# A gated cross-attention and feed-forward stack on one core: contexts loaded in whole rows, later places for two early pieces of work, smaller credits beside the attention steps

## The chip, the cores and the metric

The kernel runs on one core of a Trainium2 chip. A core has TensorE (PE, matrix products, with a path PEld that loads the fixed operand), VectorE (DVE), ScalarE (ACT), GpSimd (POOL) and SyncE (SP), and queues for DMA, which SyncE, ScalarE and GpSimd issue. The metric is the device time of one execution in microseconds (us). Three runs before the change took 3881.97, 3875.95 and 3877.2 us; the median is 3877.2. Lower is better.

## The reference

The input is x, 8 sequences of 512 tokens with 256 features, and a context of the same shape. Four blocks follow one another, each as x = x + tanh(gate) * block(layernorm(x)):

1. An mLSTM cell: queries from x, keys and values are the context itself, 8 heads of 32. Two gates come from small products of queries, keys and values. A cumulative sum of log-sigmoids gives a decay matrix; scores times decay weigh the context; a normalizer divides; a layernorm ends it.
2. Self-attention with 32 heads of 8 over each half sequence layout of the reference, then an output product, then eight experts (256 to 1024, GELU, back to 256), two per sequence here.
3. Cross-attention with 16 heads of 16: queries from x, keys and values projected from the context.
4. A product-key memory: 4096 experts found by two top-8 searches over 64 keys each; a chosen expert is one row of a down and an up table. The queries are batch-normalized over all tokens, so this block needs sums over the whole batch before it can choose.

The core of block 1, of which the context as keys and values (kh, vh) matters here:

```python
log_f = jax.nn.log_sigmoid(fg)
cs = jnp.cumsum(log_f, axis=1)
...
D_mat = jnp.exp(log_D - max_log_D)
qk = jnp.einsum('hsd,htd->hst', qh, kh) / np.sqrt(DH)
C = qk * D_mat
normalizer = jnp.maximum(jnp.abs(C.sum(axis=-1, keepdims=True)), jnp.exp(-max_log_D))
h = jnp.einsum('hst,htd->hsd', C / (normalizer + EPS), vh)
```

All is float32.

## The kernel before, in words

The first phase (`attention_phase`) does blocks 1 to 3 for all sequences; the second does block 4. TensorE's order is written out in the program and kept; in the first phase the other engines' orders are chosen by the framework's scheduler, which may bring an instruction forward when its model finds its inputs ready. A semaphore guards every true dependency.

**Steps.** The backbone of the first phase is a row of 24 attention jobs: ("A", m, f) is half f of the heads of block 2 for sequence m, ("C", m, 0) is block 3. A job has 16 steps, and a step two halves. In a half, `maxima` makes a pair of score products into a PSUM bank pair `sc` (line 417), VectorE reduces them to row maxima `nm` (line 435); for the job before it, `exponentials` makes the products the other way round, and ScalarE takes exp into `pr` (line 464). Once per step `values` multiplies by the values (line 480). Exponentials of a job begin when its maxima are closed, so two jobs run side by side, one step behind the other by a job; before the first exponentials, and in a few places later, one of the two runs alone. The score pool `ps_sc` has two buffers.

**Lanes.** Everything else of blocks 1 to 3 is cut into generators, the lanes. Between halves the planner runs pieces of lanes (`beside`): it is given a CREDIT (1.1 in the first half of a step, 2.1 in the second) and runs pieces while credit is left; what was overspent is taken off the next. A lane yields a number (the PE time of the piece it has written), or ("wait", t): not before the planner's clock `now` has moved by t, or ("rest", name): not before that name stands in `rested`, or ("take", ...) for the one accumulator bank. The clock moves after each turn by at least RETURN, 2.6 (3.9 for a step where one job runs alone, whose two halves are one turn), or by the work written. The lanes in order of precedence:
- `between` (operands of block 2's jobs: spreads of queries and keys from DRAM, lines 386 and 394, on SyncE), `values1`, `after` (leaves block 3, adds to the statistics, at the end `norm`);
- `before` for sequences 0, 2, 3, ...: `cell` (block 1) and `queries` (block 2's projections); and `behind`: `experts` and `operands` (block 3's queries); the two take turns;
- `before` for sequence 1, whose tiles are lent (`Lent`) from experts' weights, so that it runs next to the first; once the first step has begun it moves ahead of the two;
- `contexts`: block 3's keys (`keys3`, line 365 with wkv) and values (`values3`, line 376 with wkv), first for the first four sequences of the order, then for the others;
- `fill`: products of x with the down table for block 4, `ps_hd` (line 131, copied to `hb` at line 1190 and stored to `h_d`), 32 pieces a sequence, for seven sequences, each after its sequence has left block 3. The eighth sequence's products are made in the second phase.

**The start.** x of the first sequence is loaded, layernormed (lines 98 to 107; the reciprocal root `rs` is made on GpSimd, lines 103 and 104), transposed, and the gates' product `gp` (line 717) follows. A chain on VectorE and ScalarE makes the running maxima nM (to line 744), stored to DRAM (746) and read back spread over the partitions. The first sequence's cell (`all_pairs`) does all heads in a row: four such loads (line 625), a causal mask on GpSimd (638), decays on ScalarE (649), scores and their weighing (663, 669), sums with the context's keys `ce` (684), then `close` (768 to 783). Then come two layernorms, the result `xn` (888), its transposes (346), queries and keys of block 2 (365 with ws, copied at 905 and 907), its values (376, copied at 920), and through `begin` the first score.

**Context keys.** The cell's sums need the context as 8 heads of 33 columns, 32 features and a column of ones. The tile is set to ones once, and `load_keys` (line 223) loads 32 features to each head's place: per sequence four DMAs, whose contiguous pieces are 32 numbers, 128 bytes. The first sequence and sequence 1 issue them on SyncE, the other six on GpSimd.

**Waits around the change.** `Lent`'s lane loads its operands at once, and then rests on ("pairs", 0), which stands as soon as the first cell's pairs are written. `contexts` has no rest for its first half; its first piece waits 25 on the planner's clock. For its second half it rests on ("A", 1, 0).

Of the kernel before, what the change touches and what calls it, by code (L numbers as in the profile page):

```python
# [10 lines left out]
F32 = mybir.dt.float32  # L11
# [10 lines left out]
P = 128  # L22
B, S, D = 8, 512, 256
NC = S // P
# [12 lines left out]
def kernel(  # L37
# [27 lines left out]
    nc = tc.nc  # L65
# [57 lines left out]
    order = (0, 4, 1, 5, 2, 6, 3, 7)  # L123
# [56 lines left out]
    def attention_phase(ctx: ExitStack):  # L180
# [10 lines left out]
        cel, trp, wmp, wq1 = (  # L191
            early.enter_context(tc.tile_pool(name=name, bufs=bufs, side="right"))
            for name, bufs in (("cel", 2), ("trp", 1), ("wmp", 1), ("wq1", 2))
        )
# [11 lines left out]
        for c2 in range(2):  # L206
            part = slice(2 * c2, 2 * c2 + 2)
# [8 lines left out]
        cT0 = cxp.tile([P, NK, S], F32, name="cT", tag="cTc")  # L216
        nc.sync.dma_start(cT0, cxT[order[0]].rearrange("(k p) s -> p k s", p=P))
        cte = cst.tile([P, NC, WC], F32, name="cte")
        nc.gpsimd.memset(cte, 1.0)

        def load_keys(eng, ce, b):
            for c in range(NC):
                eng.dma_start(
                    ce[:, c, : 8 * 33].rearrange("p (h e) -> p h e", e=33)[:, :, 0:32],
                    cx[b, c * P : (c + 1) * P].rearrange("p (h e) -> p h e", e=32),
                )

        load_keys(nc.sync, cte, order[0])

        gwm = cst.tile([P, 4, 40], F32, name="gwm")  # L230
        nc.gpsimd.memset(gwm, 0.0)
        for i in range(2):
            part = slice(8 * i, 8 * i + 8)
# [75 lines left out]

        v0 = [cst.tile([P, NC, W0], F32, name=f"v0{f}") for f in range(2)]  # L310
        v1 = cst.tile([P, NC, W1], F32, name="v1")
        for f in range(2):
            nc.gpsimd.memset(v0[f], 1.0)
        nc.gpsimd.memset(v1, 0.0)


        m_u8 = cst.tile([B * NC, P], U8, name="m_u8")
# [3 lines left out]

        def constants():

            bo_ps = ps_m.tile([P, S], F32, name="bo_ps", tag="m")
            for k in range(NK):
                nc.tensor.matmul(
                    bo_ps[:, :D], bqkv_sb[:, 4 + k : 5 + k].to_broadcast([P, P]), wo[:, k, :],
                    start=(k == 0), stop=(k == NK - 1),
                )
            nc.vector.tensor_tensor(tbo, bo_ps[:, :D], tbo, ALU.add)  # L330
            nc.vector.tensor_scalar(tbo, tbo, tg[:, 2:3], None, ALU.mult)
            m_f = trp.tile([B * NC, P], F32, name="m_f", tag="pk", bufs=2)
            nc.vector.tensor_copy(m_f, m_u8)
            mp = ps_m.tile([P, S], F32, name="mp", tag="m")
            nc.tensor.transpose(mp[:, : B * NC], m_f, ident[: B * NC, : B * NC])
            nc.vector.tensor_copy(m_key, mp[:, : B * NC])
            nc.vector.tensor_scalar(m_f, m_f, 1.0, -NEG, ALU.subtract, ALU.mult)
            nc.sync.dma_start(m_dram, m_f)
# [211 lines left out]
        class Tiles:  # L550
# [9 lines left out]
            def begin(self, m):  # L560

                b = order[m]
                if m == 0:
                    return x0, cT0, cte
                qn = self.tokens("qn")
                self.loader.dma_start(qn, x[b].rearrange("(c p) d -> p c d", p=P))
                cT, ce = self.context(m)
                load_keys(self.loader, ce, b)
                return qn, cT, ce

            def context(self, m):
# [132 lines left out]
        def cell(m, own, loaded):  # L704
            b = order[m]
# [83 lines left out]

            if m == 0:  # L790
                all_pairs(qT, cT, ce, nM_d, aT, close)
                rested.add(("pairs", 0))
            for pair in range(4) if m else ():

                mb = own.maximum()
# [57 lines left out]
            Xa = own.stream()  # L853
# [176 lines left out]
        def contexts():  # L1030

            for half in (range(M // 2), range(M // 2, M)):
                for i in (1, 2):
                    if i == 1 and half[0]:
                        yield ("rest", ("A", 1, 0))
                    w = wsp.tile([P, NK, D], F32, name="wkv", tag="wkv")
                    nc.sync.dma_start(w, w3[i].rearrange("(k p) n -> p k n", p=P))
                    for m in half:
                        cT = load_context(m, "cT")
                        yield ("wait", 5 if m or i > 1 else 25)  # L1040
                        for cost in (keys3, values3)[i - 1](m, w, cT):
                            yield cost
                            yield ("wait", 2)
# [160 lines left out]

        LAG, CREDIT, GROUP, RETURN = 2, (1.1, 2.1), 1.1, 2.6

# [16 lines left out]
        def before(sequences, tiles):  # L1227
            own, loaded = tiles(), None
            if tiles is Lent:
                loaded = own.begin(sequences[0])  # L1230
                yield ("rest", ("pairs", 0))
            for m in sequences:
                Xa = yield from cell(m, own, loaded)
                yield from queries(m, own, Xa)
            if tiles is Lent:
                rested.add(("lent", 0))
                load_first(0)
                load_second(0)
# [106 lines left out]
        while i2 < len(steps) or pending or due:  # L1345
# [19 lines left out]
            for halves in ((0, 1),) if alone else ((0,), (1,)):  # L1365
# [18 lines left out]
                if halves[0] == 0 and pending:  # L1384
# [2 lines left out]
                        done = pending  # L1387
                    pending = None
                    used += GROUP
                new = sum(CREDIT[half] for half in halves)  # L1390
                spent = beside(credit + new)
                now += max(RETURN * (1.5 if alone else 1.0), used + new + credit - spent)
                credit = min(spent, CREDIT[1])
            if one:
                i1 += 1
                if one[1] == 15:
# [497 lines left out]
```

## Time and profile before

| what | value |
|---|---|
| median of three runs | 3877.2 us |
| profiled execution | 3878.41 us, span 3876.6 us, mean granted clock 0.966 |
| PE busy | 3534.1 us, 91% |
| DVE, ACT, POOL busy | 2247.1, 1755.9, 607.4 us |
| first score product of a step | 129.6 us |
| last exponentials | about 2937 us |
| last expert piece of the first phase | about 3015 us |
| DMA packets | 233643, of which 34558 under 512 bytes |

Times in the profile are counted from the span's start. The span is first to last instruction of the core; the profiled execution's own time is 1.8 us longer. A busy PE is modelled from instruction ends, and the granted clock tells how fast it was allowed to run: 1.00 is full, 0.50 half. A row of the timeline gives start, length, engine, line, operation, output and inputs with their shapes, how often, and in brackets the idle time before it and what ended it. SPq, POOLq and ACTq rows are DMA issues.

### The profile page before, as it was taken

What the parts mean: (1) busy time and instruction counts of PE and PEld (TensorE: products, weight loads), DVE (VectorE), ACT (ScalarE), POOL (GpSimd) and SP (SyncE); (2) the same over time, 40 slices, a digit from 0 to 9 for tenths busy, and PEclk for the clock granted to TensorE, in tenths of its full rate; (3) what the DMA queues carried; (4) which work ended last, traced back from release to release, by engine and by line L of the source; (5) the groups of instructions that cost most, each with busy time, mean ns of one, the idle gap of its engine ahead of it and who ended that gap; (6) DMA issues with size and microseconds to landing.
All of it is one profiled execution on the core that took longest, in us unless ns stands there. A gap on an engine that the chain in (4) does not pass through costs nothing. (4 is left out here: it accounts for less than half of the span.)

```text
span 3876.6 us, 76238 instructions
## 1 busy us (share of the span) xinstructions
PE 3534.1 (91%) x31049; PEld 1847.7 (48%) x31049; DVE 2247.1 (58%) x5487; ACT 1755.9 (45%) x2301; POOL 607.4 (16%) x647
## 2 busy tenths in 40 slices
PE   5788889899899999999999989979899899999998
PEld 3333334333334434443434434424345777777777
DVE  4556556546555554555554443454422589999993
ACT  2223444443444444545444544534343455555552
POOL 4113003003001200210010000010000133333331
PEclk8789999999999999999999999999999999999999
DMA  5413113123222422232232333211334432333331
GB/s 154 109 51 99 53 40 113 53 66 101 83 63 71 130 77 68 83 111 59 83 89 87 91 89 107 69 44 29 121 115 139 127 108 98 117 110 112 106 104 37
DMA packets 233643, 345.35 MB, mean 89 GB/s; under 512 B 34558, under 2 KB 182046, under 8 KB 224990
## 3 DMA queue, kind: packets, MB, share of 16 engines
q1 hardware_dynamic: 215196, 278.03, 24.3%
q0 software_dynamic: 16960, 61.87, 5.3%
q8 instruction: 244, 4.00, 0.4%
q10 hardware_dynamic: 1136, 0.58, 0.1%
q14 instruction: 107, 0.88, 0.1%
HBM read 238.50 MB, written 101.09 MB: 88 GB/s over the span
## 5 line engine op out<-in xcount | busy, mean ns | idle before, releaser
L435 DVE TENSOR_REDUCE nm<-sc 128x2 f32<-128x1024 f32 x768 | 938.9, 1225 | 988.8 <-PE sc L417 988.1
L464 ACT ACTIVATE pr<-sc 128x1024 f32<-128x1024 f32 x768 | 783.3, 1023 | 991.2 <-PE sc L417 990.7
L417 PE MATMUL sc<-ka,qa 32*128 32x512 f32 x3072 | 929.4, 667 | 155.7 <-DVE nm L435 146.5
L417 PE MATMUL sc<-qa,ka 32*128 32x512 f32 x3072 | 874.4, 655 | 16.3 <-ACT pr L464 14.6
L417 PEld LDWEIGHTS sc<-ka,qa 32*128 32x128 f32 x3072 | 253.9, 190 | 525.5 <-DVE nm L435 335.1
L1736 PE MATMUL acc<-up_sb,gs 64*128 64x256 f32 x4096 | 468.4, 382 | 1.3 <-DVE gs L1725 1.3
L131 PE MATMUL ps_hd<-xT,dw 128*64 128x256 f32 x3584 | 431.8, 387 | 11.4 <-DVE pd L839 5.3
L480 PE MATMUL av<-pr,v 128*32 128x512 f32 x3072 | 421.9, 622 | 0.0
L1736 PEld LDWEIGHTS acc<-up_sb,gs 64*128 64x128 f32 x4096 | 390.0, 187 | 52.4 <-issue 4.7
L131 PEld LDWEIGHTS ps_hd<-xT,dw 128*64 128x64 f32 x3584 | 247.6, 138 | 226.1 <-issue 86.2
L1706 POOL TENSOR_TENSOR m<-o,cwT 128x1024 f32<-128x1024 bf16 x128 | 243.6, 1903 | 583.1 <-DVE o L1704 261.2
L1190 ACT COPY hb<-ps_hd 128x512 f32<-128x512 f32 x224 | 130.9, 584 | 302.6 <-PE ps_hd L131 251.8
L417 PEld LDWEIGHTS sc<-qa,ka 32*128 32x128 f32 x3072 | 236.5, 186 | 56.0 <-ACT pr L464 41.8
L480 PEld LDWEIGHTS av<-pr,v 128*32 128x32 f32 x3072 | 61.2, 109 | 301.0 <-issue 301.0
L1725 DVE TENSOR_TENSOR gs<-cf,gs 128x1024 f32<-128x1024 f32 x128 | 155.5, 1216 | 42.3 <-PE cf L1716 27.4
L812 ACT ACTIVATE pd<-mb,aT 128x512 f32<-128x512 f32 (+1 forms) x224 | 113.3, 553 | 138.8 <-PE cav L819 71.7
L804 POOL TENSOR_SCALAR_AFFINE_SELECT mb<-mb 128x256 f32<-128x256 f32 x112 | 45.5, 407 | 781.5 <-ACT pd L812 413.5
L1716 PE MATMUL cf<-m,m 64*64 64x64 f32 x8192 | 152.9, 222 | 4.4 <-issue 3.6
L1716 PEld LDWEIGHTS cf<-m,m 64*64 64x64 f32 x8192 | 135.1, 135 | 42.6 <-issue 42.2
L1702 ACT CAST m<-o 128x1024 f32<-128x1024 bf16 x128 | 133.7, 1045 | 39.2 <-DVE o L1700 35.3
L834 PE MATMUL csc<-qT,cT 32*128 32x512 f32 (+1 forms) x448 | 125.0, 499 | 18.9 <-DVE o L508 6.0
L990 PE MATMUL ps_h<-fT,w1e 128*128 128x256 f32 x512 | 134.0, 396 | 5.8 <-DVE o L508 4.4
(260 smaller groups left out, 4058.3 us busy)
## 6 DMA issues: line engine op xcount, KB each, us to landing
h_d<-hb SPq DMA_DIRECT2D x224, 256.0 KB
gs<-h_d SPq DMA_DIRECT2D x56, 1024.0 KB
dw<-in_down SPq DMA_DIRECT2D x112, 256.0 KB
w1e<-in_w POOLq DMA_DIRECT2D x16, 1024.0 KB, 5.5
w2e<-in_w POOLq DMA_DIRECT2D x16, 1024.0 KB, 6.5
mb<-nM_d SPq DMA_DIRECT2D x28, 512.0 KB
cT<-in_cxT POOLq DMA_DIRECT2D x22, 512.0 KB, 4.9
qk_d<-pk SPq DMA_DIRECT2D x32, 256.0 KB
```

What stands on the lines that cost most here:

```text
L131: nc.tensor.matmul(ps[64 * q : 64 * q + 64, :], dw[:, k, :], runs[:, :, q, :], start=(k == 0), stop=(k == NK - 1),)
L417: nc.tensor.matmul(sc[:, i, :], lhs[r : r + 32, g, c * P : (c + 1) * P], rhs[r : r + 32, g, :], start=True, stop=True,)
L435: newest = nc.vector.tensor_reduce(self.nm[:, c, 2 * half : 2 * half + 2, g], sc, AX.X, ALU.max, negate=True)
L464: nc.scalar.activation(mine[jj], sc, AF.Exp)
L480: nc.tensor.matmul(self.av[32 * j : 32 * j + 32, :], self.va[:, c, h * (self.hd + 1) : h * (self.hd + 1) + 32], pr[j // 2][:, j % 2, :], s ...
L990: nc.tensor.matmul(ps[:, :D], w1e[:, k, f * P : (f + 1) * P], fT[:, k, i * D : (i + 1) * D], start=(k == 0), stop=(k == NK - 1),)
L1190: nc.scalar.copy(hb.rearrange("p n i t -> p i n t"), ps.rearrange("p i (n t) -> p i n t", n=2),)
L1702: nc.scalar.copy(m1, o1)
L1706: nc.gpsimd.tensor_tensor(m2, o2, tokens(cw), ALU.mult)
L1716: nc.tensor.matmul(cf[64 * q : 64 * q + 64, h, s, :], m2[rows, 4 * q + s // 2, :, s % 2], m1[rows, 4 * q + s // 2, :, s % 2], start=True, ...
L1725: nc.vector.tensor_tensor(gv, cf.rearrange("p h s i -> p i h s"), gv, ALU.mult)
L1736: nc.tensor.matmul(accs[n][q], gs[n % 2][rows, i, :], up_sb[rows, i, :], start=(i == 0), stop=(i == 63),)
```

## The change

Five things change.

1. `load_keys` makes one DMA of a whole context (rows of 256 numbers) into a staging tile, and two copies that put the features to their places between the columns of ones. The first sequence stages in a tile with the tag Xa and copies on ScalarE; the others stage in the tile that `stream()` gives (Xa again, or the lent one for sequence 1) and copy on GpSimd.
2. The memset of the first key tile goes from GpSimd to VectorE; those of v0 and v1 go from the setup into `constants()`, which is called in the first cell after the gates' product.
3. `Lent` rests on ("qk", 0), block 2's queries and keys of the first sequence, where it rested on ("pairs", 0).
4. `contexts` rests on ("begun", 0), the first step, before its first piece, and the wait of 25 is 5.
5. CREDIT is (1.0, 2.0) for (1.1, 2.1). A step in which one job runs alone still writes its two halves in one turn, but the credit is given, and the clock moved, for each half; and as long as no exponentials have run the clock moves 1.5 times as far (COLD).

```diff
-        nc.gpsimd.memset(cte, 1.0)
-        def load_keys(eng, ce, b):
-            for c in range(NC):
-                eng.dma_start(
-                    ce[:, c, : 8 * 33].rearrange("p (h e) -> p h e", e=33)[:, :, 0:32],
-                    cx[b, c * P : (c + 1) * P].rearrange("p (h e) -> p h e", e=32),
-                )
-        load_keys(nc.sync, cte, order[0])
+        nc.vector.memset(cte, 1.0)
+        def load_keys(eng, staged, ce, b, copy):
+            eng.dma_start(staged, cx[b].rearrange("(c p) d -> p c d", p=P))
+            for c2 in range(2):
+                part = slice(2 * c2, 2 * c2 + 2)
+                copy(
+                    ce[:, part, : 8 * 33].rearrange("p c (h e) -> p c h e", e=33)[:, :, :, 0:32],
+                    staged[:, part].rearrange("p c (h e) -> p c h e", e=32),
+                )
+        load_keys(
+            nc.sync, trp.tile([P, NC, D], F32, name="cx0", tag="Xa"), cte, order[0], nc.scalar.copy
+        )
...
-        for f in range(2):
-            nc.gpsimd.memset(v0[f], 1.0)
-        nc.gpsimd.memset(v1, 0.0)
...
         def constants():
+            for f in range(2):
+                nc.gpsimd.memset(v0[f], 1.0)
+            nc.gpsimd.memset(v1, 0.0)
...
-                load_keys(self.loader, ce, b)
+                load_keys(self.loader, self.stream(), ce, b, nc.gpsimd.tensor_copy)
...
                 all_pairs(qT, cT, ce, nM_d, aT, close)
-                rested.add(("pairs", 0))
...
-                        yield ("wait", 5 if m or i > 1 else 25)
+                        if m == 0 and i == 1:
+                            yield ("rest", ("begun", 0))
+                        yield ("wait", 5)
...
-        LAG, CREDIT, GROUP, RETURN = 2, (1.1, 2.1), 1.1, 2.6
+        LAG, CREDIT, GROUP, RETURN, COLD = 2, (1.0, 2.0), 1.1, 2.6, 1.5
...
-                yield ("rest", ("pairs", 0))
+                yield ("rest", ("qk", 0))
...
-                new = sum(CREDIT[half] for half in halves)
-                spent = beside(credit + new)
-                now += max(RETURN * (1.5 if alone else 1.0), used + new + credit - spent)
-                credit = min(spent, CREDIT[1])
+                for half in halves:
+                    spent = beside(credit + CREDIT[half])
+                    spell = max(
+                        RETURN * (0.75 if alone else 1.0), used + CREDIT[half] + credit - spent
+                    )
+                    now += spell if i2 else COLD * spell
+                    credit, used = min(spent, CREDIT[1]), 0.0
```

## The prediction

> **What bounds the kernel now.** I read the page, then the busy times by 100 us, then the timeline of the first 130 us, then the expert products and the steps by window. The page gives the bound, TensorE, and who makes it wait.
>
> ```profile
> span 3876.6 us, 76238 instructions
> PE 3534.1 (91%) x31049; PEld 1847.7 (48%) x31049; DVE 2247.1 (58%) x5487; ACT 1755.9 (45%) x2301; POOL 607.4 (16%) x647
> ...
> L417 PE MATMUL sc<-ka,qa 32*128 32x512 f32 x3072 | 929.4, 667 | 155.7 <-DVE nm L435 146.5
> ```
>
> PE is idle 342 us in all, of which it spends 146.5 waiting for VectorE to empty the score bank (nm, L435). The busy times by window show where the rest is (columns: window, length, PE, PEld, DVE, ACT and POOL busy, granted clock, DMA share, GB/s):
>
> ```profile
> 0.00:100.00 100.00, 58.18 (x257) 31.41 (x257) 49.95 (x124) 29.14 (x51) 41.50 (x62) 0.83 0.55 152
> 100.00:200.00 100.00, 74.93 (x267) 36.63 (x268) 52.20 (x87) 22.03 (x43) 11.83 (x30) 0.72 0.39 104
> 200.00:300.00 100.00, 86.03 (x418) 33.62 (x420) 60.49 (x107) 30.21 (x49) 12.60 (x28) 0.87 0.17 58
> ...
> 2100.00:2200.00 100.00, 96.97 (x608) 46.06 (x608) 47.57 (x59) 49.69 (x52) 2.34 (x3) 1.00 0.22 69
> ...
> 2500.00:2600.00 100.00, 82.81 (x544) 33.62 (x542) 52.44 (x64) 41.54 (x44) 13.79 (x13) 0.98 0.22 61
> 2600.00:2700.00 100.00, 86.25 (x508) 37.62 (x508) 50.23 (x63) 47.03 (x47) 1.71 (x2) 0.97 0.11 28
> 2700.00:2800.00 100.00, 83.54 (x521) 37.38 (x520) 49.29 (x71) 33.65 (x38) 4.71 (x5) 0.93 0.32 103
> ```
>
> Two thin places: the first 300 us (81 us idle, and a low clock), and 2500 to 2800 (47 idle, against 3 to 9 in each 100 us from 2000 to 2500). The expert products ps_hd (one piece is 16 matmuls, 1.95 us) explain the second; columns here are PE, PEld, ACT, clock, DMA:
>
> ```profile
> 2500.00:2600.00 100.00, 9.52 (x80) 5.39 (x80) 2.91 (x5) 0.98 0.22 61
> 2600.00:2700.00 100.00, 0.00 (x0) 0.00 (x0) 0.00 (x0) 0.97 0.11 28
> ```
>
> By 2560 the 160 pieces of the first five sequences are used up; the sixth waits for the block that leaves at about 2780. The timeline tells the start:
>
> ```profile
> 8.10 1.07 POOL L594 MEMSET cte<- 128x1180 f32 x1
> 10.13 0.25 POOL L103 TENSOR_SCALAR ln_rs<-ln_mv 128x4 f32<-128x4 f32 x1
> 38.72 0.42 SPq L625 DMA_DIRECT2D qa<-nM_d  x1
> 41.06 0.44 POOL L638 TENSOR_SCALAR_AFFINE_SELECT qa<-qa 128x256 f32<-128x256 f32 x1
> 83.23 5.36 PE L365 MATMUL ps_p<-cT,wkv 128*128 128x256 f32 x16 [5.47 <-DMA cT<-in_cxT]
> 85.36 1.38 DVE L888 TENSOR_SCALAR xn<-Xa,ln_mv,rs 128x256 f32<-128x256 f32 x4 [2.74 <-POOL rs L885]
> 98.45 0.60 PE L346 MATMUL ps_t<-ident,xn 128*128 128x128 f32 x4
> 104.62 10.06 PE L365 MATMUL ps_p<-nT,ws 128*128 128x256 f32 x32
> 129.60 1.31 PE L417 MATMUL sc<-ka,qa 32*128 32x512 f32 x2
> ```
>
> xn is ready at 86.74, but PE takes it up at 98.45: in its written order stand the second cell's transposes and gate products (88 to 93.6) and block 3's keys, which wait for their contexts. The first score is at 129.60; 384 steps of two halves follow, until 2937.
>
> **The start, step by step.** The sum is made in the profiled execution: 3878.4 us, 1.8 around its span; the median of the runs is 1.2 under it.
> - Memsets. The first layernorm's ln_mv is done at 7.46, its rs waits on GpSimd until 10.13 behind memsets of v0, v1 and both cte (0.62 twice, 1.04, 1.08, 1.07); all but the last leave the place, one of them for VectorE, idle until 5.77. Gain 2.7 at most; I take 2.5.
> - SyncE's queue. The first context's loads issue for 5.75 us and the second cell's for 5.02, in 128-byte pieces; a whole 512 KB load issues in 0.42 (qn at 23.73). nM is ready at 30.35, stored at 31.19. The second, third and fourth maxima loads (38.72, 41.14) stand behind the two stores of block 3's keys. The first lands after 7.2 us; later such loads land after 4.2 (182.76 to 186.92) to 7.7 (123.70 to 131.45). Gain 0 to 4.5 for the first; up to 3 more for the later ones (selects wait for them at 47.80 and 49.06). I take 4.
> - Two casts of 0.75 for block 3's keys leave VectorE between 76 and 79: 1.5.
> - xn to nT: 11.7 us of queue go, and of the 5.0 from there to 103.44 some 1 to 2, since the second cell's scan (1.20) and cast lie between the two halves. I take 13.
> - From the projections' end, 114.7, to 129.60: csc of the second cell stands ahead of the first score and waits for a vk copy (128.77), which waits for a v_d store. Between 3 worse and 4.6 better; I take 2.
>
> New waits here: ScalarE's two copies of the first context wait for its load; behind them on its queue stand five small loads (b1 to tbo, issued by 6.6 before) of which the first use is at 9.54 (lns) and 24.55 (tbo), so some 2 us late costs nothing; if ScalarE held until 15, its cast of qT (14.28) would slip by 1 to 2. GpSimd's load of Xa (10.32) has to wait for those copies, as Xa is their room, and rs may stand behind it: 0 to 2. GpSimd's two copies for the second cell wait for a load on SyncE issued near 24; behind them come the selects of the first cell, at 41.06 before, far enough.
>
> So the first score comes about 23 us earlier, at 107 (bounds 9 and 30).
>
> The clock: every row after a gap shows 0.50 (25 to 35, 80 to 85, 105 to 110), and 16 products take 3.69 us at 1.00 but 5.36 to 6.19 where part is at 0.50. With block 3's keys gone PE is emptier before the first cell and before the projections; all 32 at half clock would be 12.4 instead of 10.06 (twice the 6.19 row). I take 0, and keep 2.3 in the range. The Trainium skill, page TensorE: Matmul & The Clock Gate, section What's actually happening, speaks against this part too: the clock falls to half after about 3.4 us of idleness and returns after as much work; by that the projections cost half of 3.4, 1.7, where the sum has 0.
>
> **What was moved comes back.** Four keys3 (4 x 3.69) and the second cell's head (transposes 1.3, gates 3.8, at 1.0, first csc some 1.2): 22 us of PE, now beside steps, with 8 casts of 0.75, 8 stores on SyncE, and context loads on GpSimd. Cover: PE is idle 121 us between 100 and 1000, where no expert product is there yet. What a piece costs is read from half-steps of the timeline. An empty half lasts 2.5 us (2654.58 to 2657.06, with values; 2658.65 to 2661.11, without). With 1.99 us of a lane it lasts 3.0 (2642.45 to 2645.45), with values too 4.0 (1214.54 to 1218.53). So 1.99 us costs 0.5 to 1.5, half on the mean: 11 us (bounds 0, 22).
>
> The second cell now starts later, while its keys are wanted 23 us earlier: its last spread issues at 363.8, the next job's first reduce is at 369.8, a margin of a few us. Against that, waits told in planner time end in 1.5 times fewer steps before the first exponentials (COLD), and its lane comes first once steps run. I take 4 us (bounds 0, 25: five steps with one stream at about 5).
>
> **Smaller credits.** 3.0 for 3.2 per step. A piece of credit 1.8 is 1.95 us, so 0.22 us of lane work leaves a step, and from 1000 to 2560, 225 steps, 49 us: 25 pieces. Where PE is at 93 to 97% the step shortens by as much and nothing is won. But the 25 pieces are then left for 2560 to 2800, where the idle time above a usual stretch (5.4 per 100) is 11.8 + 8.3 + 11.0 = 31. I take 20, since C7's operands still come late there (bounds 0, 31). Whatever is left later runs after the steps: 14 pieces took 28.4 us from 2986, 2.03 each, no worse. Against it, a smaller credit may leave more halves empty: between 300 and 1000 a half has 1.44 us of lane and 0.35 idle, between 1000 and 2390 1.65 and 0.23; on that slope 0.11 us less is 0.067 more idle per half, 51 us over 768. The two stretches hold other pieces, though; with pieces of 1.8 the halves fill about as before, and I take 0 (bounds -10, +51).
>
> **Contexts of the other cells.** Six times four GpSimd issues of 0.90, 3.6 us, become one of 0.9 and two copies of 128x512: a memset of 128x2048 takes 1.79, a select of 128x256 0.41, so 0.5 to 1.2 each. GpSimd is busy 16%. The copies wait there for the landing (3.2 to 5.7) and for the last cell's products, as the issues did (79 us in all); behind them are rs of the layernorms and selects. 0, bounds -2 and +6. The skill's GPSIMD Engine Reference, section Engine selection, calls one-input work there roughly line rate, but it shares its SBUF interface with VectorE; no row here shows what that costs.
>
> **Sum:** -23 + 11 + 4 - 20 = -28: 3849.
>
> **Rivals.**
> 1. As summed: 3849, 3828 to 3866. Chance 0.51.
> 2. The start alone: the pieces left over go to the end of the steps and the thin stretch stays: -8, 3869 (3858 to 3880). For: C7 waits there for a chain of waits, not for work. Chance 0.19.
> 3. The second cell is late and the score stream stalls for five steps or more: +21 on the sum, 3870 (3858 to 3885). For: the margin at 364. Against: COLD. Chance 0.10.
> 4. Slower: the smaller credit leaves halves empty, 0.058 us more idle (most of that slope) in each of 768, +45: 3894 (3878 to 3908). It decides from 28/768 = 0.036 us per half. For: PE's 146.5 us on nm; against: rows of 1.07 us of lane that cost nothing. Chance 0.20.
>
> 0.2% is 7.7 us, about what a measurement of this kernel tells. Below 3869.5: 0.50 of case 1, 0.10 of 2, 0.04 of 3: 0.64. Above 3885: 0.01, 0.01, 0.04 and 0.17: 0.23. The rest, 0.13. The range 3822 to 3892 leaves out some 0.06 below and 0.13 above.
>
> **What would show it.** The first score at 98 to 120; rs at 7.5 to 8; no key projection before it. PE over 90% from 2500 to 2800, with pieces of ps_hd in each 100 us. Idle per half in 1000 to 2400 still 0.20 to 0.26. A(1,0)'s first reduce within 8 us of the last of A(0,1). Wrong: an unchanged start, a gap in the reduces near step 32, or idle per half over 0.26.

## The result: no change that can be measured

The changed kernel takes 3876.9 us in the median of 20 runs, the kernel before 3875.0 in 20 runs beside them. The ratio is 1.0007, with a 95% interval of 0.9996 to 1.0019. The forecast was 3849; the range held the time, the forecast itself did not: 28 us were to be won and none were.

Yet the start that the prediction described can be seen: the first score, the reciprocal root and the keys' place are as forecast. Of the other signs that it named, the idle time per half is as forecast, the thin place is not over 90% busy in each 100 us, and a gap in the reduces near step 32, its sign of being wrong, is there. Two lines of the page and the start of the changed kernel, from its timeline (line numbers after the change are up to 10 higher: 422 is 417, 370 is 365, 892 is 888):

```profile
span 3878.1 us, 76212 instructions
PE 3526.9 (91%) x31049; PEld 1841.5 (47%) x31049; DVE 2247.9 (58%) x5491; ACT 1756.9 (45%) x2300; POOL 597.9 (15%) x642
...
L422 PE MATMUL sc<-ka,qa 32*128 32x512 f32 x3072 | 918.9, 663 | 129.9 <-DVE nm L440 105.7
```

```profile
7.74 0.23 POOL L103 TENSOR_SCALAR ln_rs<-ln_mv 128x4 f32<-128x4 f32 x1 [0.86 <-DVE ln_mv L102]
19.31 0.23 DVE L338 CAST m_f<-m_u 32x128 f32<-32x128 uint8 x1 [7.05 <-DMA m_u<-in_mask]
19.46 1.36 DVE L107 TENSOR_SCALAR qn<-qn,ln_mv,ln_rs 128x256 f32<-128x256 f32 x4
43.03 0.41 POOL L643 TENSOR_SCALAR_AFFINE_SELECT qa<-qa 128x256 f32<-128x256 f32 x1 [11.39 <-DMA qa<-nM_d]
83.41 1.38 DVE L892 TENSOR_SCALAR xn<-Xa,ln_mv,rs 128x256 f32<-128x256 f32 x4 [2.73 <-POOL rs L889]
83.97 2.21 PE L351 MATMUL ps_t<-ident,xn 128*128 128x128 f32 x8 [13.21 <-DVE xn L892]
86.23 9.35 PE L370 MATMUL ps_p<-nT,ws 128*128 128x256 f32 x32
107.53 4.43 PE L422 MATMUL sc<-ka,qa 32*128 32x512 f32 x8 [3.19 <-DMA ka<-qk_d]
```

The first score is at 107.53, forecast 107. The reciprocal root is on GpSimd at 7.74. PE takes up xn 0.56 us after VectorE begins it, for 13.1 before (85.36 to 98.45). But VectorE's layernorm comes at 19.46, 7.2 later than before: in VectorE's queue it stands behind a cast that waits for the mask. In the kernel before, the cast was not ahead of it:

```profile
12.26 1.46 DVE L107 TENSOR_SCALAR qn<-qn,ln_mv,ln_rs 128x256 f32<-128x256 f32 x4 [1.73 <-POOL ln_rs L104]
```

So 20 of the 22 us of lead come from behind xn, which itself begins 2.0 earlier, and the layernorm that the memsets were to bring forward gives none of it. PE's wait for VectorE to empty the score bank (the last column of the page's line) falls from 146.5 to 105.7 us, and the kernel is no faster for it.

The thin place before the end, by 100 us from 2500 (window, length, busy PE, PEld, DVE, ACT, POOL, clock, DMA share, GB/s), and then the expert products ps_hd alone in the same windows (PE, PEld, ACT):

```profile
2500.00:2600.00 100.00, 95.48 (x706) 42.25 (x708) 44.05 (x54) 40.72 (x51) 13.10 (x12) 0.97 0.33 99
2600.00:2700.00 100.00, 87.98 (x516) 38.43 (x509) 50.10 (x60) 48.11 (x48) 1.70 (x2) 0.97 0.12 33
2700.00:2800.00 100.00, 81.01 (x554) 36.46 (x552) 44.83 (x68) 36.36 (x43) 4.71 (x5) 0.95 0.36 114
```

```profile
2500.00:2600.00 100.00, 40.38 (x320) 21.92 (x320) 11.44 (x20) 0.97 0.33 99
2600.00:2700.00 100.00, 0.00 (x0) 0.00 (x0) 0.28 (x1) 0.97 0.12 33
2700.00:2800.00 100.00, 13.19 (x112) 7.60 (x112) 3.99 (x7) 0.95 0.36 114
```

Pieces are left for 2500 to 2600 (20 where 5 were), and that slice fills from 82.81 to 95.48. The next one has again none and hardly moves (86.25 to 87.98), and the third falls from 83.54 to 81.01.

And the gap that the prediction kept as its third rival is there. PE's waits between 355 and 402 in the changed kernel (total, times, longest):

```profile
PE sc L422 <- DMA qa<-nm_sb: 11.9, 1, 11.9
PE sc L422 <- DMA ka<-qk_d: 8.5, 1, 8.5
```

A(1,0)'s first reduce starts 47.0 us after the last of A(0,1); before it was 2.8. How the lead ran along the attention jobs (start of the first maxima reduce of a job, from the timeline, us):

| job | before | after | lead |
|---|---|---|---|
| A(0,0) | 133.9 | 111.6 | 22.3 |
| A(0,1) | 236.2 | 225.7 | 10.5 |
| A(1,0) | 369.8 | 401.8 | -32.0 |
| C(1,0) | 1060.4 | 1047.5 | 12.9 |
| A(5,1) | 1860.8 | 1818.5 | 42.3 |
| C(5,0) | 2531.1 | 2506.9 | 24.2 |
| C(6,0) | 2616.8 | 2610.9 | 5.9 |
| start of the last exponential | 2937.0 | 2935.0 | 2.0 |

So the time isn't lost where the gap is: 650 us later the kernel is ahead. But it is ahead mostly on credit, with pieces of the lanes put off. Counted as in the ledger below, PE has done as much work as before by 1047.5 (less by 0.6 us) and 11 us more by 1818.5, where the leads are 12.9 and 42.3. By 2500 it has made 140 expert pieces, the kernel before 155; 15 at 1.95 us are 29 us of PE that it still owes, and its lead at C(5,0) is 24. By 2600 both have made all 160 that are there to be made, and 6 us of lead are left.

A ledger of the profiled executions, worked out from the trace: PE's idle time, and what PE lost to the clock (busy time times one less the clock granted while it ran), in us. PE's work at full clock is the same within 20 us in all kernels here (3411 to 3431); the difference is in these two columns.

| window | before | after | after less before |
|---|---|---|---|
| 0 to 110 | 44.9 + 13.4 | 56.9 + 11.1 | +9.7 |
| 110 to 250 | 30.7 + 30.1 | 23.8 + 32.5 | -4.5 |
| 250 to 400 | 23.0 + 12.1 | 35.7 + 10.8 | +11.4 |
| 400 to 1500 | 102.8 + 34.3 | 90.6 + 23.7 | -22.8 |
| 1500 to 2500 | 59.1 + 8.5 | 67.5 + 13.6 | +13.5 |
| 2500 to 2800 | 47.4 + 10.4 | 35.5 + 8.4 | -13.9 |
| rest | 34.8 + 4.7 | 41.1 + 10.1 | +11.7 |
| all | 343 + 113 | 351 + 110 | +5 |

The start ends 22 us sooner, but from 0 to 110 PE idles 12 us more than before, and still 4 more if each kernel is counted up to its own first score (56.9 up to 107.5, 52.9 up to 129.6). The start was not filled better. Work was taken out of it, and that work was still to be done.

### The profile page after: what moved, and what is told of

Its sections match the earlier page's. It is cut to its first block, busy times and chain, and to the rows that moved or that the text cites. A ratio compares the mean times of both kernels' runs of the same rounds, so it can differ in the third digit from the quotient of the medians.

```text
span 3878.1 us, 76212 instructions
## 1 busy us (share of the span) xinstructions
PE 3526.9 (91%) x31049; PEld 1841.5 (47%) x31049; DVE 2247.9 (58%) x5491; ACT 1756.9 (45%) x2300; POOL 597.9 (15%) x642
## 2 busy tenths in 40 slices
DMA packets 226090, 345.34 MB, mean 89 GB/s; under 512 B 25982, under 2 KB 174494, under 8 KB 217438
## 5 line engine op out<-in xcount | busy, mean ns | idle before, releaser
L422 PE MATMUL sc<-ka,qa 32*128 32x512 f32 x3072 | 918.9, 663 | 129.9 <-DVE nm L440 105.7
L1735 DVE TENSOR_TENSOR gs<-cf,gs 128x1024 f32<-128x1024 f32 x128 | 155.7, 1217 | 42.2 <-PE cf L1726 27.4
L1712 ACT CAST m<-o 128x1024 f32<-128x1024 bf16 x128 | 133.7, 1045 | 39.5 <-DVE o L1710 35.7
```

Source lines behind the costliest of these rows:

```text
L422: nc.tensor.matmul(sc[:, i, :], lhs[r : r + 32, g, c * P : (c + 1) * P], rhs[r : r + 32, g, :], start=True, stop=True,)
L1712: nc.scalar.copy(m1, o1)
L1735: nc.vector.tensor_tensor(gv, cf.rearrange("p h s i -> p i h s"), gv, ALU.mult)
```

## Experiments

Eighteen kernels, each timed beside the kernel before. "us" is the ratio less one, times 3874. "Planner" is part 5 of the change (credits, clock by halves, COLD), "keys" part 4, "second" part 3, "loads" parts 1 and 2. The intervals reach 4 to 9 us to either side, so a difference of two rows is good to some 10 us.

| kernel | ratio, 95% interval | us |
|---|---|---|
| after: the full change | 1.0007 [0.9996, 1.0019] | +3 |
| e1: after, second cell at its old place | 1.0060 [1.0039, 1.0080] | +23 |
| e2: after, mask loaded first | 1.0020 [1.0003, 1.0037] | +8 |
| e3: after, old credits | 1.0125 [1.0103, 1.0148] | +48 |
| e15: after, old clock | 1.0043 [1.0027, 1.0060] | +17 |
| e4: loads | 1.0018 [1.0005, 1.0032] | +7 |
| e5: planner | 0.9950 [0.9932, 0.9967] | -19 |
| e8: planner, loads | 0.9956 [0.9943, 0.9969] | -17 |
| e14: planner, loads, mask first | 0.9975 [0.9961, 0.9988] | -10 |
| e9: planner, keys | 1.0043 [1.0031, 1.0056] | +17 |
| e13: planner, second | 1.0124 [1.0105, 1.0143] | +48 |
| e10: planner, keys, second | 1.0003 [0.9988, 1.0018] | +1 |
| e12: clock and COLD | 0.9962 [0.9947, 0.9977] | -15 |
| e11: credits (1.0, 2.0) | 0.9891 [0.9873, 0.9909] | -42 |
| e20: credits (1.0, 2.0), memsets | 0.9906 [0.9885, 0.9927] | -36 |
| e19: credits (0.95, 1.95) | 0.9887 [0.9867, 0.9906] | -44 |
| e16: credits (0.9, 1.9) | 1.0022 [1.0011, 1.0034] | +9 |
| e17: credits (1.05, 2.05) | 1.0014 [1.0004, 1.0024] | +5 |
| e18: credits (1.2, 2.2) | 1.0078 [1.0063, 1.0093] | +30 |

### The full change with one part put back

e1 puts the second cell's rest back:

```diff
                 all_pairs(qT, cT, ce, nM_d, aT, close)
+                rested.add(("pairs", 0))
...
-                yield ("rest", ("qk", 0))
+                yield ("rest", ("pairs", 0))
```

> The changed kernel, with the second cell resting on (pairs, 0) again, as before the change; block 3's keys stay behind the first step. Theory A (the second cell's late start is what ate the gain): the gap of 47 us in the reduces before A(1,0) shrinks to under 8, A(1,0) begins near 350, and the time is 3830 to 3850. Rival B (the lead of the start is lost further down in any case, since C7's operands and the last pieces set the end): the gap goes, but the time stays at 3870 to 3880.

The gap ahead of A(1,0) goes (47.0 to 2.7), and the kernel is slower, by 0.5%, outside the ranges of both theories. The gap is not what eats the gain.

e2 loads the mask on ScalarE's queue, ahead of the weights:

```diff
-        m_u8 = cst.tile([B * NC, P], U8, name="m_u8")
-        nc.sync.dma_start(m_u8, mask)
...
+        m_u8 = cst.tile([B * NC, P], U8, name="m_u8")
+        nc.scalar.dma_start(m_u8, mask)
         gb_sb = cst.tile([40, 1], F32, name="gb_sb")
```

> The changed kernel, with the mask loaded on ScalarE's queue ahead of the weights. Theory A': VectorE stood at the cast of the mask (19.31, 7 us after the mask's load) and held the first layernorm behind it; with the mask early the layernorm's result comes near 10 to 12 in place of 19.5, the first reduce near 104 in place of 111.6, and the time falls by 0 to 8 us to 3869 to 3877, less if the second cell still holds A(1,0). Rival: another load holds VectorE or the gates' product, and the first reduce stays within 2 us of 111.6.

The layernorm moves from 19.46 to 13.37, the first reduce only from 111.6 to 109.4, near what the rival said, and the end not at all.

e3 takes the smaller credits out (first pair of lines), e15 the new clock (the rest):

```diff
-        LAG, CREDIT, GROUP, RETURN, COLD = 2, (1.0, 2.0), 1.1, 2.6, 1.5
+        LAG, CREDIT, GROUP, RETURN, COLD = 2, (1.1, 2.1), 1.1, 2.6, 1.5
...
-                for half in halves:
-                    spent = beside(credit + CREDIT[half])
...
-                    now += spell if i2 else COLD * spell
-                    credit, used = min(spent, CREDIT[1]), 0.0
+                new = sum(CREDIT[half] for half in halves)
+                spent = beside(credit + new)
+                now += max(RETURN * (1.5 if alone else 1.0), used + new + credit - spent)
+                credit = min(spent, CREDIT[1])
```

> The changed kernel with credits of 1.1 and 2.1 again (still given per half, clock as in the change). Theory A (the smaller credit gains 20 to 40 us, by filling 2500 to 2600 and by shorter halves, and hides the loss at the second cell): 3895 to 3915, with PE idle again over 12 us in 2500 to 2600. Rival C (the credit is neutral; the lanes only move): 3870 to 3882.

> The full change with the planner's old clock (no COLD, one turn for a step with one job); the credits stay (1.0, 2.0). Theory N, the new clock takes 22 us from the credits wherever both are: 3850 to 3858 (0.993 to 0.996). Theory O, the clock isn't to blame inside the full change, the keys' later place is: 3870 to 3885. Rival: without COLD the waits of the lanes end later, the gap ahead of A(1,0) grows beyond the 47 us of the full change, and it is slower: above 3890.

Inside the full change the credits are worth 45 us (48 less 3), more than theory A's range, and the clock 14 (17 less 3). Theory A's sign is missing in e3: from 2500 to 2600 PE idles 4.7 us, not over 12. So there the credits don't act by filling the thin place: from 2500 to 2800 idle time and clock loss are 50.9 us in e3 and 43.9 in the changed kernel, 7 of the 43.3 between their spans. Theory N, that the clock takes 22 us from the credits wherever both are, is refuted. Without COLD the gap ahead of A(1,0) is 94.7 us instead of 47.0, as the rival said, but the median, 3887.4, falls between the ranges of theory O and of the rival.

### Parts alone

e4 has the loads and the moved memsets alone, e5 the planner part, e8 both; e14 adds the mask's place (e2's diff) to e8. The core of e4's edit and of e5's, each against the kernel before:

```diff
-        nc.gpsimd.memset(cte, 1.0)
+        nc.vector.memset(cte, 1.0)
...
-            for c in range(NC):
-                eng.dma_start(
...
+            eng.dma_start(staged, cx[b].rearrange("(c p) d -> p c d", p=P))
+            for c2 in range(2):
...
-                load_keys(self.loader, ce, b)
+                load_keys(self.loader, self.stream(), ce, b, nc.gpsimd.tensor_copy)
```

```diff
-        LAG, CREDIT, GROUP, RETURN = 2, (1.1, 2.1), 1.1, 2.6
+        LAG, CREDIT, GROUP, RETURN, COLD = 2, (1.0, 2.0), 1.1, 2.6, 1.5
...
-                new = sum(CREDIT[half] for half in halves)
-                spent = beside(credit + new)
...
+                for half in halves:
+                    spent = beside(credit + CREDIT[half])
...
+                    now += spell if i2 else COLD * spell
```

> The kernel before with the whole-row loads, their copies and the moved memsets alone. The planner's part alone is 19 us faster than before, and with loads and the later keys added (the second cell as before) 24 slower: 43 us lie in those two parts. Theory D (the later place of block 3's keys costs them): within 8 us of before. Rival E (the loads cost them, by a staging tile shared with the cell's end and by VectorE held at the mask's cast): 15 to 40 us slower.

> The kernel before with the planner's part of the change alone: credits 1.0 and 2.0, given and clocked per half, clock 1.5 times before the first exponentials. Theory A: faster by 15 to 35 us (3842 to 3862), with pieces of ps_hd in 2500 to 2600. Rival C: within 6 us of before. The fourth rival of the prediction (empty halves): slower by 10 to 40 us, idle per half over 0.26 from 1000 to 2390.

> The kernel before with the planner's part and the loads. Theory D: near the planner's part alone, 3845 to 3860. Rival E: 3875 to 3895.

> The planner part and the whole-row loads, with the mask loaded on ScalarE's queue ahead of the weights, so that VectorE's queue isn't held at the mask's cast. The planner part with the loads was at 3857 (0.9956), the planner part alone at 3851 (0.995); there the first reduce was at 120.8 and 113.7. Theory A, the start's lead reaches the end where nothing new fills it: first reduce at about 114, total 3848 to 3852. Theory B, a few us at the start are lost again in the steps, as in the full change with the mask first: 3855 to 3860.

The loads cost 7 us alone and 2 beside the planner part, the last within the noise. That is theory D, not E: of the 43 us between e1 and e5 the loads have little, and the keys' later place has 36 (see the two moves). In e4 VectorE's layernorm is late as in the full change:

```profile
18.59 0.21 DVE L338 CAST m_f<-m_u 32x128 f32<-32x128 uint8 x1 [6.02 <-DMA m_u<-in_mask]
18.73 1.36 DVE L107 TENSOR_SCALAR qn<-qn,ln_mv,ln_rs 128x256 f32<-128x256 f32 x4
```

In e14 the mask is no longer ahead of it, and it is later still: the scheduler now puts the second cell's statistics there, which wait for x (19.45). A wait that is taken away at the head of a queue leaves its place to the next:

```profile
19.45 1.41 DVE L98 BATCH_NORM_STATS2 ln_st<-qn 128x6 f32<-128x256 f32 x4 [5.89 <-DMA qn<-in_x]
20.77 0.36 DVE L102 BATCH_NORM_AGGREGATE ln_mv<-ln_st 128x2 f32<-128x6 f32 x4
21.05 1.36 DVE L107 TENSOR_SCALAR qn<-qn,ln_mv,ln_rs 128x256 f32<-128x256 f32 x4
```

e14's first reduce, at 119.7, is not the 114 of theory A, and its median, 3861.2, is just above theory B's range. The planner part alone has its first reduce at 113.7, 20 us earlier than the kernel before, and is faster by 0.5%, as theory A said. So most of the lead that the prediction gave to the moves comes from the planner's order. It is a move all the same: the first keys' products run from 74.1 to 98.2 in the kernel before, and from 71.5 to 165.6 in e5, where the other clock puts a part of them behind the first score (e12, the clock alone, does so too; with e11's credits alone all of them start ahead of it).

### The two moves

e9 adds the keys' later place to the planner part (first lines), e13 the second cell's (last two), e10 both (which is the full change without loads and memsets):

```diff
-                        yield ("wait", 5 if m or i > 1 else 25)
+                        if m == 0 and i == 1:
+                            yield ("rest", ("begun", 0))
+                        yield ("wait", 5)
...
-                yield ("rest", ("pairs", 0))
+                yield ("rest", ("qk", 0))
```

> The kernel before with the planner's part and block 3's keys behind the first step, loads and second cell as before. Theory D: 3880 to 3895, first reduce near 111, and the first job's maxima take 130 us or more in place of 98. Rival E: 3845 to 3860.

> The planner part and the second cell behind block 2's queries and keys; block 3's keys stay where they were, and so do the loads. Putting the second cell back took 15 to 20 us on top of the later keys, in spite of a gap of 47 us ahead of A(1,0). Theory H, its later place is a gain by itself: 3851 less 15, about 3836 (0.991). Theory I, it is a gain only where the late keys crowd the first steps, and alone the gap ahead of A(1,0) costs: 3858 to 3880 (0.996 to 1.001), with A(1,0) starting 20 us or more behind the end of A(0,1).

> The whole change without its loads and memsets: planner, keys behind the first step, second cell behind the first projections. Theory D: like the whole change, 3868 to 3882, with the gap before A(1,0). Rival E: 3840 to 3860.

The keys' later place costs 36 us (17 for -19). The second cell's costs 67 alone (48 for -19) and wins 16 once the keys are later (1 for 17), 20 in the full change (after against e1). Turned round, the keys' later place wins 47 once the second cell is later (1 for 48). So neither price belongs to one move by itself; both together cost 20 (1 for -19), though e10's first reduce, at 105.4, is 8.3 us ahead of e5's. e9 and e10 are in the ranges of theory D. e13 has the gap ahead of A(1,0) that theory I named (37.4 us), but at +48 it is outside both theories' ranges; and the gap is no measure of the price, as e10 has it too (47.9). One reading is that the first steps have room for one of the two, since the first job lasts 102.3 us in the kernel before (A(0,0) to A(0,1)), 131.6 in e5, 140.3 in e9 and 112.5 in e10. But in e13, where nearly all of the first keys' products stand ahead of the first score, it lasts 136.0, which this doesn't explain, and no run measures that room by itself.

Part of the keys' 36 us goes with the clock of their new place. PE between 150 and 165 in e9 (columns as above: PE, PEld, DVE, ACT, POOL, clock):

```profile
150.00:155.00 5.00, 4.75 (x17) 2.21 (x18) 1.58 (x3) 0.78 (x2) 0.00 (x0) 0.50 0.00 0
155.00:160.00 5.00, 5.00 (x16) 1.82 (x15) 4.01 (x5) 0.00 (x0) 0.00 (x0) 0.50 0.00 0
160.00:165.00 5.00, 5.00 (x15) 1.94 (x12) 2.02 (x5) 1.60 (x4) 0.41 (x1) 0.50 0.00 0
```

and the keys' products between 60 and 420, first in e5, then in e9 (duration of one: least, median, most; first and last start):

```profile
L365 PE MATMUL ps_p<-cT,wkv x48: 379/379/794, 71.5 to 165.6; 128*128 128x256 f32 x48
```

```profile
L365 PE MATMUL ps_p<-cT,wkv x64: 379/634/797, 130.3 to 256.5; 128*128 128x256 f32 x64
```

All products of that line between 60 and 420 sum to 60.1 us in e5 (144 of them) and 78.1 in e9 (160; 16 more at 0.379 are 6): 12 us more for the same work. The larger part of the difference between these two profiles, whose spans are 45.2 us apart, comes later, in idle time and clock loss from 600 to 1000 (65.1 for 42.1) and from 1500 to 2000 (58.5 for 42.2). From 600 to 1000 PE waits longer for VectorE to empty the score bank (33.9 us for 19.3), and the cells run late (the fourth sequence's xn at 690.1 for 625.6). Which of these makes the other is not shown.

### What in the planner part makes the gain

e11 changes nothing but the two numbers, e12 everything else of part 5:

```diff
-        LAG, CREDIT, GROUP, RETURN = 2, (1.1, 2.1), 1.1, 2.6
+        LAG, CREDIT, GROUP, RETURN = 2, (1.0, 2.0), 1.1, 2.6
```

> The kernel before with the credits (1.0, 2.0) and nothing else: the planner's clock is the old one. The whole planner part took 19 us off (ratio 0.995) and brought the first reduce from 133.9 to 113.7. Theory F, the smaller credits make the gain: 3855 to 3862, ratio 0.995 to 0.997, a half from 1000 to 2390 at 3.43 for 3.50. Theory G, the clock by halves and COLD make it: within 6 us of the kernel before. The first reduce tells by itself which of the two leads at the start: at 114 it is the credits, at 134 the clock. Theory K, the parts work only together: this one at 3885 or slower.

> The kernel before with the clock by halves and COLD, and the old credits (1.1, 2.1). Theory F: no gain, and as the old credits inside the full change cost 46 us, perhaps a loss: 3875 to 3920. Theory G: 3855 to 3862. Theory K, only together: above 3890. The first reduce is at 114 if the clock by halves and COLD make the lead at the start, at 134 if the credits do.

The credits alone win 1.1%, more than theory F said; the clock alone wins 0.4%, about what theory G said of it (3854.2 for 3855 to 3862); so neither theory holds, and K doesn't either; together they win 0.5%, so the clock costs 23 us on top of the credits. Of the lead at the start (20.2 in e5), the credits alone bring 9.3 (first reduce at 124.6) and the clock alone 14.9 (119.0). In e11 the thin place is filled, in part as the prediction meant it:

```profile
2500.00:2600.00 100.00, 91.66 (x688) 37.21 (x692) 49.01 (x55) 44.58 (x52) 10.94 (x9) 1.00 0.28 79
2600.00:2700.00 100.00, 88.38 (x517) 42.27 (x513) 48.37 (x69) 46.80 (x48) 5.15 (x5) 0.98 0.10 33
2700.00:2800.00 100.00, 92.27 (x689) 38.48 (x691) 44.46 (x56) 43.94 (x53) 1.27 (x2) 1.00 0.44 143
```

From 2500 to 2800 its idle time is 27.7 for 47.4 and its clock loss 1.7 for 10.4. The first slice has 14 pieces of ps_hd for 5, left over as forecast. The second has none, as before. The third has 16 for 4, not left over: they are the sixth sequence's, which begin at 2741 for 2789. Over all, idle time and clock loss are 316 + 90 for 343 + 113, 50 us, and its profiled span is 50.2 shorter. Where the lead of the full change at C(5,0) was owed, here 49.2 us of lead stand against 9 pieces, 18 us, and 36.1 are left at C(6,0).

e5 and e11 stand level at C(7,0) (2705.1 and 2705.4); e5's last exponential starts 11.1 us later and its last expert piece 15.4. So of what the clock costs beside the credits, the larger part is lost after 2700, not in the early steps for which it was written.

### Four more sizes

Only the two numbers of the credits differ, as in e11's diff.

> The kernel before with credits (1.2, 2.2). Theory L: slower by 20 to 50 us, 3895 to 3925 (1.005 to 1.013), with a half from 1000 to 2390 longer than 3.50 and the expert products used up before 2560. Theory M: anywhere, and as likely faster than slower.

> The kernel before with credits (1.05, 2.05). Theory L: half the gain of (1.0, 2.0), 3845 to 3857 (0.992 to 0.995). Theory M: anywhere between 3830 and 3900, and as likely above the kernel before as below it.

> The kernel before with credits (0.95, 1.95). Theory L2, one curve: the lead grows with a smaller credit until the lanes no longer bring a job's operands in time. Then C(4,0) starts between 2023 and 2037 (0.9: 2027, 1.0: 2033), and the gaps ahead of A(7,0) and C(7,0) are between those of 1.0 (3.5 and 19.3) and of 0.9 (52.9 and 72.2): total 3825 to 3860. Theory M, chance: C(4,0) anywhere between 2000 and 2090, and the total with it.

> The kernel before with credits (0.9, 1.9). Theory L, the credits act by their size: another 20 to 45 us, 3785 to 3810 (0.977 to 0.984), or, if halves now run empty, back up to 3840 with idle per half from 1000 to 2390 over 0.25. Theory M, any change of the number reshuffles: anywhere between 3800 and 3900, without order among the sizes.

First the readings along the jobs:

| credits | C(4,0) starts | gap ahead of A(7,0) | ahead of C(7,0) | pieces by 2500 | last piece of the phase | us |
|---|---|---|---|---|---|---|
| 1.2, 2.2 | 2129.9 | 2.7 | 15.2 | 154 | 3046.4 | +30 |
| 1.1, 2.1 | 2083.2 | 2.7 | 17.5 | 155 | 3015.1 | 0 |
| 1.05, 2.05 | 2073.2 | 3.5 | 19.6 | 150 | 3006.0 | +5 |
| 1.0, 2.0 | 2033.0 | 3.5 | 19.3 | 146 | 2970.6 | -42 |
| 0.95, 1.95 | 2014.0 | 3.5 | 68.5 | 134 | 2959.4 | -44 |
| 0.9, 1.9 | 2027.4 | 52.9 | 72.2 | 120 | 3020.1 | +9 |

(Gaps are from the start of one reduce to the start of the next; inside a job 2.5 to 3.5 is usual.) The start of C(4,0) falls with the credit down to 0.95. Below that the lanes bring the operands too late. In the kernel with 0.9 PE's waits from 2253 to 2306 name the loads of A(7,0):

```profile
PE sc L417 <- DMA ka<-qk_d: 6.7, 1, 6.7
PE sc L417 <- DMA qa<-nm_sb: 2.3, 1, 2.3
```

and the last cell's xn, which has to come before them, is at 2244.9, where 1.0 has 2119.7. So there is a dose, with a turning point, and not chance alone. But it is no straight line. From 1.1 to 1.05 nothing is won where theory L had half of the gain (1.0014; e17's profiled execution, to which its row belongs, is the fastest of its 11, 3867.2), and from 1.05 to 1.0 come 47 us; C(4,0) of 0.95 is 9 us earlier than theory L2 allowed, and the total of 0.9 is 40 above what L had for empty halves (idle time per maxima reduce from 1000 to 2390 is 0.27, over the 0.25 that L named for that case). The pieces are whole, so a small change of the number moves some of them past a step and others not; how much of the 47 is that, these runs don't tell.

### The memsets

e20 is e11 with the memsets moved:

```diff
-        nc.gpsimd.memset(cte, 1.0)
+        nc.vector.memset(cte, 1.0)
...
-        for f in range(2):
-            nc.gpsimd.memset(v0[f], 1.0)
-        nc.gpsimd.memset(v1, 0.0)
...
         def constants():
+            for f in range(2):
+                nc.gpsimd.memset(v0[f], 1.0)
+            nc.gpsimd.memset(v1, 0.0)
```

> The kernel before with credits (1.0, 2.0), and with the memsets moved: the first key tile's to VectorE, v0's and v1's to constants(). The loads and the lanes' places are the old ones. By the forecast's term: rs on GpSimd at 7.5 to 8 for 10.13, qn on VectorE at 9.7 to 10.3 for 12.27, and 2.5 us off the credits' 3829: 3825 to 3828. Rival: the start's lead of 2.5 us is not passed on, or the constants' memsets, now in GpSimd's queue ahead of the first selects, hold those: first select at 41 or later, 3829 to 3834.

rs starts 2.5 us earlier, and its second instruction then waits behind one of the moved memsets:

```profile
7.63 0.23 POOL L103 TENSOR_SCALAR ln_rs<-ln_mv 128x4 f32<-128x4 f32 x1 [0.75 <-DVE ln_mv L102]
7.82 0.64 POOL L322 MEMSET v<- 128x668 f32 x1
8.44 1.04 POOL L104 TENSOR_TENSOR ln_rs<-ln_rs,eps 128x4 f32<-128x4 f32 x1
```

The layernorm gains 1.1 (11.16 for 12.26), the first select is at 41.70 (39.47 in e19, whose start is the old one), and the time, 3831.7, is that of e11 within the intervals, as the rival said.

The fastest kernels of the study are those with nothing but smaller credits: 3829.0 us with (1.0, 2.0) and 3823.8 with (0.95, 1.95), which can't be told apart. Both beat the kernel before and the changed one by 1.1%.

## Why the prediction was wrong, step by step

- **"The start", -23.** Its size was right (22.1 at the first score), two of its terms were not. The memsets' 2.5 and SyncE's 4 were to bring the first select 6.5 us forward; it came 2.0 later (43.03 for 41.06). The text looked for what stands behind GpSimd and SyncE and not for what stands ahead in VectorE's queue, which is ordered by the scheduler and not by the program. xn to nT was given 13; from xn to the projections it is 16.4 (19.26 before, 2.82 after). The real fault is that the lead was entered as time won: at the first step it was work put off. And e5 has 20.2 of it by the planner part alone; moves, loads and memsets together add 2 at the first reduce (113.7 to 111.6).
- **"What was moved comes back", +11, bounds 0 and 22.** This is the step that failed most. With the second cell at its old place the keys' later place costs 36 us, outside the bounds; the two moves together cost 20 (e10 against e5), their lead at the start included. The price was read from half-steps after 1200, in stretches of 100 us whose clock is 0.97 to 0.98 (one of its empty halves, 2658.65 to 2661.11, itself ran at 0.83); the moved pieces run from 130 to 257, where e9's clock is 0.66 on the mean (110 to 250). The row that gave this away was shown: 0.72 for 100 to 200. The keys' products take 12 us more there; the rest of the 36 comes later and its cause stays open.
- **"The second cell", +4, bounds 0 and 25, and rival 3.** The stall was there, 47 us in A(1,0), more than the five steps of the rival. Its price was not: put right (e1), the kernel is slower by 20, while without the keys' later place the same move costs 67 (e13). A stall of the score stream isn't by itself lost time: lanes that would have to run anyway can run in it.
- **"Smaller credits", -20.** Too small, and right in mechanism only in part: 42 alone, 45 in the full change. Alone, the thin place gives 28 (20 of idle time, 9 of clock, as worked out), and 19 are won before 2500, where the text entered nothing. In the full change the thin place gives 7 (e3), and the rest comes earlier. Rival 4 is refuted: idle time per maxima reduce from 1000 to 2390 is 0.225 in the changed kernel and 0.236 in e11, for 0.232 before, where the rival needed 0.058 more.
- **COLD and the clock by halves** were taken for a help to the second cell only. They win 15 alone and 14 in the full change, and cost 23 beside the credits.
- **Contexts of the other cells, 0.** Not measured apart from the first cell's loads and the memsets. Together these cost 7 alone and 2 beside the other parts, where the sum had 0 here and -6.5 in the start.
- **Rival 2, the start alone.** Its time, 3869, was near, its reason was not: the thin place did fill in part, and the start was what gave nothing.

Along the chain e5, e9, e10, after the parts are: planner part -19, keys +36, second -16, loads and memsets +2. They make the measured +3 by construction; with the second cell first, it would be +67 for it and -47 for the keys. The forecast put -23 + 11 + 4 against the last three, -8 in all, where they measure +22 in either order; its -20 for the planner part was right by luck, as credits and clock win 42 and 15 alone and lose 38 of that together.

The rule that the Trainium skill gives in TensorE: Matmul & The Clock Gate, section What's actually happening, is that the clock falls after about 3.4 us of idleness and comes back after as much sustained work. The changed kernel's two waits ahead of A(1,0) fit it roughly: PE stops at 358.4 and 390.3, the clock is at half from 360.3 to 374.0 and from 394.5 to 404.7, so it falls 1.9 and 4.2 us into the waits of 11.9 and 8.5 us, and is back 3.7 and 6.0 us after they end. e9 does not fit: its clock falls at 106.6 and at 147.6, with no wait of PE over 2.6 us in the 10 us before, and in the three rows of e9 above PE is busy 14.75 of 15 us while the clock stays at 0.50 throughout, 20.5 us in all (147.6 to 168.0).

## What to carry to other kernels

Work that is moved out of a start has to be paid where it lands, at the clock of that place; take the price from rows there, and count a lead as won only when idle time has gone, not when a mark comes earlier. Where a planner orders the work, parts of a change don't add: the same edit won 16 us in one company and cost 67 in another, so try the smallest part alone before the whole. A size that has an optimum is to be scanned on both sides, and the place where its curve turns (here operands that come too late) is read from the gaps in the stream that it feeds.

## What the runs showed of the hardware

Two things were not expected. TensorE's clock stayed at half for 20 us though the engine had work for 98% of that time (19.51 of 20 us from 150 to 170 in e9; the clock is back at 168.0); from 151.3 to 163.9 these are products of the forms 32*128 and 128*64, but no run varied that. And the whole-row loads, which bring the packets under 512 bytes from 34558 to 25982 and each context's issues from four to one, left no gain in the time: +7 us alone.
